# Layer 0 of a graph network with a new order: sums two blocks ahead of the neighbour lists, group steps half a block apart

## The chip, the cores and the metric

The kernel runs on one core of a Trainium2 chip. The metric is the device time of one execution in microseconds (us); lower is better. The engines are PE (TensorE), DVE (VectorE), ACT (ScalarE) and POOL (GpSimd); SP only issues DMAs. Each engine works through its own instructions strictly in the order of the program, and waits for the others by semaphores.

## The reference

Four layers over one graph with 3327 nodes, 256 features and a random adjacency matrix (int32, about 16 neighbours a row).

```python
# layer 0
h = x @ Wt.T + bt                                   # 3327 x 64
s = leaky_relu(h @ Wa.T + ba, 0.2)                  # one score per row
w = softmax(where(adj > 0, s, NEG), axis=1)         # the score of a row is the same for all its neighbours
y = x + (w @ h) @ Wp.T + bp
x = gamma * (y - mean) * rsqrt(var + eps) + beta
# layers 1 to 3
q, k, v = layer_norm(x, g1, be1) @ w_qkv            # 8 heads of 32
x = x + softmax(where(adj, q k / sqrt(32), -inf)) v @ w_proj + b_proj
x = x + gelu(layer_norm(x, g2, be2) @ w1 + b1) @ w2 + b2
```

## The kernel before, in words

Rows are handled in 26 blocks of 128 (`NB`; the last has 127), blocks in 7 groups of four (the last group has two). Everything below happens in layer 0 (`sparse_path`, lines 623 to 1131); layers 1 to 3 follow and gather the neighbours' keys and values row by row with indirect DMAs (L1226). They need two things from layer 0: the table `t1` (rows and neighbour lists) and `perm`, the rows sorted by number of neighbours, by which `t1` is read (L1186).

Per **block** (class `Block`):
- `load` (L696): 1.66 MB of the adjacency matrix go to `a32` (three buffers, DMA on SP); ACT's `sign` (L705) turns them into bf16 `abf` (three buffers), POOL sets the pad columns (L702).
- `turn` (L707): 26 transposes on PE in four chunks (L714), each chunk copied to `aT` by ACT (L715). There are two PSUM buffers for the chunks, and `aT` holds a pair of blocks.
- `candidates` (L717): DVE multiplies `abf` by column numbers (L720) and takes the eight largest of each of 16 segments (L724).
- `list` (L726): DVE takes the 40 largest of these 128 (L735, L737): the neighbour list.

`setup` (L740) turns the weights, brings x to h through PE (`x_turn` L767, `h_of` L779), splits h into three bf16 parts (L805 to L809), and makes the column sum of h (L817, `phsum`) and the scores s (L823 to L827). x itself is loaded by 26 indirect DMAs on POOL (L658).

Per **pair**, `sums` (L838): 52 matmuls of 256 columns add h over the neighbours of 256 rows.

Per **group** (class `Group`) twelve steps: `copy` (L853, ACT), `back` (L860, PE and ACT: sums and degrees with rows on partitions), `soft` (L871, DVE: degrees, one-hot `OH` of the degree, the row's rank among rows of equal degree through PE's `places`, softmax factors; its two exponentials are on ACT, L911), `mix` (L915, DVE), `project` (L933, PE; the bias bp is a matmul with K=1, L944), `add` (L950, DVE: residual, statistics, an inverse root in thirteen small operations), `norm` (L960, DVE), `norm1` (L969, DVE statistics for layer 1), `turn1` (L974, ACT and PE), `qkv(0)` and `qkv(2)` (L982, PE and ACT, two blocks each), `store` (L999, DMA to `t1` on ACT's queue).

Most PSUM results go through `bank`, a pool of three. The order is written out by hand: everything runs in program order, so where a step is called decides where it stands in the queue of each of its engines. In the main loop (L1032 to L1049) a block is loaded one block ahead, turned, then (for even i) the pair before is summed, and then the steps in the list `late` are called one or two at a time between `candidates` and `list`:

```python
turn(i)
if i == 0:
    S.w1 = load_qkv(1, a, bank); setup()
elif i % 2 == 0:
    sums(i - 1)
k = 1 if i < NB - 2 else 2
some(k); blk[i].candidates(); some(k); blk[i].list(); some(k)
```

After the loop comes the sort (L1052 to L1105): prefix sums over degrees (`more`), the rank of each row, its high and low digits (`hib`, `lo`), one-hot matrices (L1089 to L1095) and 26 matmuls (L1098) that give `perm`. The last group's steps stand among and behind it (L1049, L1069, L1075, L1087, L1108). `norm1` uses `Norm` (L566), whose `scale` ends in `nm` (L582) and whose `turn` (L588, L591) and `out` (L596) make the transposed, normalised x.

Of the kernel before, what the change touches and what calls it, by code (L numbers as in the profile page):

```python
# [523 lines left out]
def sparse_path(ctx, tc, ins, out, dram, flag):  # L524
# [98 lines left out]
    with tc.tile_pool(name="a", bufs=1) as a, tc.tile_pool(name="aw", bufs=2) as aw, \  # L623
# [42 lines left out]
        nrow = 3 * D + 2 * H0 + 1  # L666
        row = a.tile([1, nrow], FP, name="s_row")
        o = 0
        for name, n in (("gamma", D), ("beta", D), ("bp", D), ("bt", H0), ("Wa", H0), ("ba", 1)):
            src = ins[f"L0_gnn_{name}"]  # L670
            nc.sync.dma_start(row[:, o:o + n], src if len(src.shape) == 2 else src[None, :])
            o += n
# [15 lines left out]
        places = a_acc.tile([P, 512], FP, tag="places", name="places")  # L688

        class Block:  # L690
# [5 lines left out]
            def load(self):  # L696
                i, r = self.i, self.r
                a32 = aw.tile([P, N], I32, tag="a32", bufs=3, name=f"s_a32_{i}")
                for p0, p1 in (((0, P),) if r == P else ((0, r // 16 * 16), (r // 16 * 16, r))):
                    nc.sync.dma_start(a32[p0:p1], ins["adj"][i * P + p0:i * P + p1, :])  # L700
                self.abf = aw.tile([P, PADDED], BF, tag="abf", bufs=3, name=f"s_abf_{i}")
                nc.gpsimd.memset(self.abf[:, N:], 0.0)  # L702
                if r < P:
                    nc.gpsimd.memset(self.abf[96:P, :], 0.0)
                nc.scalar.sign(self.abf[:r, :N], a32[:r])  # L705
# [11 lines left out]
            def candidates(self):  # L717
                i = self.i
                v = aw.tile([P, NSEG, SEG], BF, tag="v", name=f"s_v_{i}")
                nc.vector.tensor_mul(v, self.abf.rearrange("p (s c) -> p s c", c=SEG),  # L720
                                     seg1[:, None, :].to_broadcast([P, NSEG, SEG]))
                self.cand = aw.tile([P, NSEG, 8], FP, tag="cand", name=f"cand_{i}")
                for s in range(NSEG):
                    nc.vector.max(out=self.cand[:, s, :], in_=v[:, s, :])  # L724
# [15 lines left out]
        def setup():  # L740

            wtT = a.tile([P, 2, H0], FP, name="s_wtT")
            S.wpT = a.tile([H0, D], FP, name="s_wpT")
# [5 lines left out]
            nc.vector.tensor_copy(wtT, pt[:, :2 * H0].rearrange("p (c h) -> p c h", c=2))  # L749
            nc.vector.tensor_copy(S.wpT, pt2[:H0, :D])  # L750
# [7 lines left out]
            S.gam_b, S.bet_b, S.bp_b = (brow[:, k * D:(k + 1) * D] for k in range(3))  # L758
            bt_b = brow[:, 3 * D:3 * D + H0]
            wa_b = brow[:, 3 * D + H0:3 * D + 2 * H0]  # L760
            ba_b = brow[:, nrow - 1:nrow]

            h_sb = aw.tile([P, NB, H0], FP, tag="abf", bufs=3, name="s_h")
            nc.vector.memset(h_sb[96:P, NB - 1, :], 0.0)
            turned = {}

            def x_turn(g):  # L767
                blocks = GROUPS[g]
                xT = aw.tile([P, 2, 512], FP, tag="hT", name=f"s_xT_{g}")
                for c in range(2):  # L770
                    pb = bank(f"s_px_{g}_{c}")
                    for j, i in enumerate(blocks):
                        nc.tensor.transpose(pb[:, j * P:(j + 1) * P],
                                            x_sb[:, i, c * P:(c + 1) * P], ident)
                    (nc.vector.tensor_copy if c else nc.scalar.copy)(
                        xT[:, c, :len(blocks) * P], pb[:, :len(blocks) * P])
                turned[g] = xT

            def h_of(g):  # L779
                blocks, xT = GROUPS[g], turned.pop(g)  # L780
                ph = bank(f"s_ph_{g}").rearrange("p (b h) -> p b h", h=H0)
                for j, i in enumerate(blocks):
                    for c in range(2):
                        nc.tensor.matmul(ph[:, j, :], xT[:, c, j * P:(j + 1) * P],
                                         wtT[:, c, :], start=(c == 0), stop=(c == 1))
                full = [j for j, i in enumerate(blocks) if ROWS[i] == P]
                for j0, j1, r in ((0, len(full), P), (len(full), len(blocks), ROWS[-1])):
                    if j1 > j0:
                        i0 = blocks[j0]
                        nc.vector.tensor_add(  # L790
                            h_sb[:r, i0:i0 + j1 - j0, :], ph[:r, j0:j1, :],
                            bt_b[:r, None, :].to_broadcast([r, j1 - j0, H0]))

            for g in range(len(GROUPS)):
                x_turn(g)
                if g:
                    h_of(g - 1)
            h_of(len(GROUPS) - 1)

# [3 lines left out]
            nc.vector.tensor_copy(hs[:, :, :H0], h_sb)  # L805
            nc.vector.tensor_sub(rest, h_sb, hs[:, :, :H0])
            nc.vector.tensor_copy(hs[:, :, H0:2 * H0], rest)
            nc.vector.tensor_sub(rest, rest, hs[:, :, H0:2 * H0])
            nc.vector.tensor_copy(hs[:, :, 2 * H0:3 * H0], rest)  # L809
            S.fold = a.tile([P, H0], FP, name="s_fold")  # L810
            nc.vector.tensor_copy(S.fold, ident[:, :H0])
            nc.vector.tensor_add(S.fold, S.fold, ident[:, H0:])

            ph = bank("s_phsum")
            for i in range(NB):
                r = ROWS[i]
                nc.tensor.matmul(ph[:, :H0], ones[:r, :], h_sb[:r, i, :],  # L817
# [4 lines left out]

            nc.vector.tensor_mul(rest, h_sb, wa_b[:, None, :].to_broadcast([P, NB, H0]))  # L823
            s = S.s = a.tile([P, NB], FP, name="s_s")
            nc.vector.tensor_reduce(s, rest, AX.X, ALU.add)
            nc.vector.tensor_scalar(s, s, ba_b, None, ALU.add)
            nc.vector.scalar_tensor_tensor(s, s, 0.2, s, ALU.mult, ALU.max)  # L827

        class Group:
# [17 lines left out]

            def steps(self):
                return [self.copy, self.back, self.soft, self.mix, self.project, self.add,
                        self.norm, self.norm1, self.turn1, lambda: self.qkv(0),  # L850
                        lambda: self.qkv(2), self.store]
# [19 lines left out]
            def soft(self):  # L871
# [4 lines left out]
                def sv(name):  # L876
# [10 lines left out]
                                        top[:, :, None].to_broadcast([P, n, nd]), ALU.is_equal)  # L887
                for j in range(n):
                    i = b0 + j
                    nc.tensor.matmul(places[:, :nd], tri, OH[:, i, :], start=(i == 0), stop=True,  # L890
                                     skip_group_check=True)
                    t = aw.tile([P, nd], FP, tag="place", name=f"place_{i}")
                    nc.vector.tensor_mul(t, places[:, :nd], OH[:, i, :])
                    nc.vector.tensor_reduce(rank[:, i:i + 1], t, AX.X, ALU.add)
                    nc.tensor.matmul(places[:, :nd], rest_tri, OH[:, i, :], start=False, stop=True,
                                     skip_group_check=True)
# [36 lines left out]
            def project(self):  # L933
# [4 lines left out]
                nT = aw.tile([H0, 512], FP, tag="nT", bufs=1, name=f"s_nT_{g}")  # L938
                nc.scalar.copy(nT[:, :n * P], pt[:H0, :n * P])
                self.ps = []  # L940
                for j0 in range(0, n, 2):
                    ps = bank(f"s_pp_{g}_{j0}").rearrange("p (b d) -> p b d", d=D)
                    for j in range(2):
                        nc.tensor.matmul(ps[:, j, :], ones[0:1, :], row[:, 2 * D:3 * D],  # L944
                                         start=True, stop=False)
# [622 lines left out]
```

## Time and profile before

| | us |
|---|---|
| median of 3 runs | 2890.99 (2877.77 to 2891.98) |
| profiled execution | 2888.34 |
| its span, first to last instruction | 2886.5 |
| mean granted clock of PE over the span | 0.816 |
| first neighbour list begins (L720) | 75.60 |
| list of block 25 ends | 566.4 |
| perm is written (L1105) | 611.8 |
| first gather from t1 (L1186) | 630.1 |
| busy from 0 to 612: PE, DVE, ACT | 364, 415, 224 |

A span is read from the first to the last instruction of one execution; busy time is the time in which an engine runs instructions; the granted clock says which share of its full speed PE had. A window's row gives the busy time of PE, PE's weight loads, DVE, ACT and POOL with the number of instructions, then the clock, the share of the 16 DMA engines and GB/s. A wait is an engine's idle time before an instruction, with the engine and line that ended it, the total, how often and the longest.

### The profile page before, as it was taken

Reading aid. Unit: us, or ns where it says so; the run is one execution under the profiler, and the core shown is the slowest. Engines: PE = TensorE matmul, PEld = TensorE weight load, DVE = VectorE, ACT = ScalarE, POOL = GpSimd, SP = SyncE. Lnnn points to the kernel's source line nnn. Section 1 sums busy time; section 2 is a strip of 40 time slices with the busy share of each in tenths; the row PEclk is TensorE's granted clock in tenths of the full one; section 3 lists DMA queues with packets and bytes.
Section 4 is the critical chain, followed back from the end, with each engine's and each line's share of the span. In section 5 each row is a group of like instructions: output and inputs, shape, how many; then the busy total and the mean of one; then the engine's idle time right before and its main releaser. Section 6 shows DMA issues by size and latency. Waiting matters only on the chain. (4 is left out here: it accounts for less than half of the span.)

```text
span 2886.5 us, 21905 instructions
## 1 busy us (share of the span) xinstructions
PE 2003.6 (69%) x6391; PEld 1062.0 (37%) x6391; DVE 1981.0 (69%) x4141; ACT 791.8 (27%) x1363; POOL 1359.1 (47%) x1461
## 2 busy tenths in 40 slices
PE   4566666623678887897347878878782678777866
PEld 4344444411334333344213434333350233333334
DVE  2977787447787777773378877777714886778852
ACT  2443443200233332332102323332230023222221
POOL 3000000017776766650377655665405777777740
PEclk9677666756889989898678989988995798888988
DMA  4323331137776766670477656665506776666650
GB/s 179 128 98 119 125 104 52 52 112 217 217 220 197 210 197 188 181 180 16 144 210 210 194 174 178 190 181 155 120 27 189 210 202 194 190 190 188 200 135 15
DMA packets 144480, 453.67 MB, mean 157 GB/s; under 512 B 29522, under 2 KB 40157, under 8 KB 141022
## 3 DMA queue, kind: packets, MB, share of 16 engines
q0 software_dynamic: 113056, 370.26, 45.7%
q1 hardware_dynamic: 9834, 53.90, 5.3%
q10 hardware_dynamic: 21458, 28.02, 2.7%
q8 instruction: 52, 0.85, 0.1%
q14 instruction: 80, 0.65, 0.1%
HBM read 420.64 MB, written 31.42 MB: 157 GB/s over the span
## 5 line engine op out<-in xcount | busy, mean ns | idle before, releaser
L1226 POOL DMA_INDIRECT kv<-kv,t x1344 | 1273.2, 947 | 806.0 <-issue 370.0
L1294 PE MATMUL po<-vw,s_ident 128*128 128x512 f32 (+1 forms) x1380 | 778.2, 700 | 493.5 <-DVE vw L1289 443.6
L1248 DVE TENSOR_TENSOR kv<-kv,q 128x1024 f32<-128x1024 f32 (+3 forms) x363 | 413.4, 1139 | 309.7 <-DMA kv<-kv,t 152.9
L1294 PEld LDWEIGHTS po<-vw,s_ident 128*128 128x128 f32 x1380 | 286.3, 221 | 845.3 <-issue 476.5
L1249 DVE TENSOR_REDUCE sc<-kv 128x32 f32<-128x1024 f32 (+3 forms) x363 | 414.1, 1141 | 12.4
L1289 DVE TENSOR_TENSOR vw<-kv,w 128x1024 f32<-128x1024 f32 x333 | 371.2, 1127 | 0.2
L1373 PE MATMUL pu<-fT,s_w 128*128 128x512 f32 (+3 forms) x768 | 302.4, 527 | 1.0 <-ACT fT L596 1.0
L1396 PE MATMUL py<-gT,s_w 128*128 128x512 f32 (+2 forms) x672 | 283.8, 549 | 0.0
L1379 ACT ACTIVATE gT<-pu,pvb 128x512 f32<-128x512 f32 (+3 forms) x192 | 116.6, 608 | 350.7 <-PE pu L1373 350.2
L702 POOL MEMSET s_abf<- 128x1 bf16 x26 | 2.6, 104 | 435.2 <-PE s_ptb L714 251.6
L1373 PEld LDWEIGHTS pu<-fT,s_w 128*128 128x128 f32 x768 | 147.4, 201 | 136.2 <-issue 111.6
L1396 PEld LDWEIGHTS py<-gT,s_w 128*128 128x128 f32 x672 | 127.8, 192 | 123.1 <-issue 105.4
L714 PE MATMUL s_ptb<-s_ident_bf,s_abf 128*128 128x128 bf16 x676 | 76.5, 291 | 115.7 <-ACT s_aT L715 84.4
L724 DVE MAX8 cand<-s_v 128x8 f32<-128x208 bf16 x416 | 117.5, 360 | 0.9
L714 PEld LDWEIGHTS <-s_abf 128*128 128x128 bf16 x676 | 65.4, 135 | 128.9 <-issue 94.7
L1426 PE MATMUL pk<-s_w_qkv,nT 128*128 128x512 f32 x208 | 106.4, 636 | 8.8 <-ACT nT L596 8.8
L588 ACT ACTIVATE xn_f<-t,nm_f,rqy_f 128x256 f32<-128x256 f32 x78 | 42.9, 593 | 247.6 <-DVE nm_f L582 238.3
L1263 ACT ACTIVATE sc<-sc,mx 128x120 f32<-128x120 f32 (+6 forms) x78 | 31.9, 410 | 260.9 <-DVE mx L1260 257.1
L1334 DVE TENSOR_TENSOR t<-t,po 128x256 f32<-128x256 f32 x78 | 32.5, 417 | 99.7 <-PE po L1330 95.2
L715 ACT COPY s_aT<-s_ptb 128x896 bf16<-128x896 bf16 x104 | 83.3, 853 | 64.6 <-PE s_ptb L714 64.6
L1186 POOL DMA_INDIRECT t<-t,perm x26 | 24.6, 946 | 158.6 <-DMA colsb<-in_L_gnn_be_dram 151.0
L1414 DVE TENSOR_TENSOR t<-t,pd 128x256 f32<-128x256 f32 x75 | 29.5, 408 | 93.3 <-PE pd L1410 93.3
(285 smaller groups left out, 2455.0 us busy)
## 6 DMA issues: line engine op xcount, KB each, us to landing
s_a<-in_adj_dram SPq DMA_DIRECT2D x25, 1663.5 KB
kv<-kv,t POOLq DMA_INDIRECT x1344, 3.8
kv<-kvr ACTq DMA_DIRECT2D x52, 256.0 KB
kv<-s_kvr ACTq DMA_DIRECT2D x26, 256.0 KB
s_w<-in_L_gnn_w_dram SPq DMA_DIRECT2D x6, 1024.0 KB
t<-ql ACTq DMA_DIRECT2D x6, 592.0 KB
t<-s_x ACTq DMA_DIRECT2D x6, 512.0 KB
s_w_qkv<-in_L_gnn_w_qkv_dram SPq DMA_DIRECT2D x3, 768.0 KB
```

Of the source, the lines that this page charges most:

```text
L714: nc.tensor.transpose(pt[:, m, :], self.abf[:, k * P:(k + 1) * P], ident_bf)
L715: nc.scalar.copy(aT[:, k0:k0 + len(ks), :], pt[:, :len(ks), :])
L724: nc.vector.max(out=self.cand[:, s, :], in_=v[:, s, :])
L1226: nc.gpsimd.indirect_dma_start(out=t[:, s, :], out_offset=None, in_=kv[L], in_offset=bass.IndirectOffsetOnAxis(ap=t2[:, b, k:k + 1].bitcas ...
L1248: nc.vector.tensor_mul(k, k, self.q[b][:, None, :].to_broadcast([P, n, D]))
L1249: nc.vector.tensor_reduce(self.sc[b][:, s0:s0 + n, :], k.rearrange("p s (h d) -> p s h d", d=HD), AX.X, ALU.add)
L1289: nc.vector.tensor_mul(vw[:, :n * D].rearrange("p (s h d) -> p s h d", h=HEADS, d=HD), v, self.wp[b][:, s0:s0 + n, :, None].to_broadcast([ ...
L1294: nc.tensor.matmul(self.po[b][:, :m], ident, vw[:, s * D:s * D + m], start=(s0 + s == 0), stop=(s0 + s + 2 >= S), skip_group_check=True)
L1373: nc.tensor.matmul(c["pu", f][:, :n], w["w1"][:, e, f * P:(f + 1) * P], c["hT"][:, e, :n], start=(e == 0), stop=(e == 1))
L1379: nc.scalar.activation(g[:, :n], c.pop(("pu", f))[:, :n], AF.Gelu_apprx_tanh, bias=w["b1"][:, f:f + 1])
L1396: nc.tensor.matmul(c["py"][e][:, :n], w["w2"][:, f, e * P:(e + 1) * P], g[:, :n], start=(f == 0), stop=last)
L1426: nc.tensor.matmul(ps[:, :c1 - c0], c["hT"][:, e, j * P:(j + 1) * P], nxt["w_qkv"][:, e, c0:c1], start=(e == 0), stop=(e == 1))
```

## The change

Layer 0 computes the same, with these edits.

- **Start.** Blocks 0 to 2 are loaded, signed and turned first; blocks 0 and 1 get their lists before the weights are turned. `setup` is split into `weights0`, `split_h` and `of_h`; the turns of x are called with pieces of the candidates and lists of blocks 2 and 3 between them. h lies in an `a32` buffer instead of an `abf` buffer. The pad columns of the first three blocks are set on DVE.
- **Lead.** In round i block i+2 is loaded, signed and turned, and the pair that ends with i+2 is summed, while block i gets its list.
- **Group steps by a plan.** A table gives the half round in which each step is called; steps are mostly one half round apart, with two from `back` to `soft`.
- **soft.** The four blocks of a group are ranked with one product and one sum over 4 x 41 columns; PE adds up all earlier blocks' counts (`ones_bf`, `rest_tri`) into four regions of `places`, which are cleared once by a matmul with zeros.
- **norm** is done by ACT in one instruction per block; gamma and beta follow on DVE, once per group, in `norm1`.
- **bp** becomes a 65th row of the projection weights, with a row of ones in `nT`; the K=1 matmuls go. Some copies (`wtT`, `wpT`, half of `xT`) go from DVE to ACT.
- **End.** The last group's `soft`, `mix` and `project` are in the last round; `add`, `norm`, `norm1`, `turn1`, `qkv` and `store` are placed before the one-hot part of the sort.

```diff
-                nc.scalar.sign(self.abf[:r, :N], a32[:r])
+            def sign(self):
...
+                (nc.vector if i < 3 else nc.gpsimd).memset(self.abf[:, N:], 0.0)
...
+                nc.scalar.sign(self.abf[:r, :N], self.a32[:r])
...
                 for j in range(n):
                     i = b0 + j
-                    nc.tensor.matmul(places[:, :nd], tri, OH[:, i, :], start=(i == 0), stop=True,
-                                     skip_group_check=True)
-                    t = aw.tile([P, nd], FP, tag="place", name=f"place_{i}")
-                    nc.vector.tensor_mul(t, places[:, :nd], OH[:, i, :])
-                    nc.vector.tensor_reduce(rank[:, i:i + 1], t, AX.X, ALU.add)
-                    nc.tensor.matmul(places[:, :nd], rest_tri, OH[:, i, :], start=False, stop=True,
-                                     skip_group_check=True)
+                    add = [(tri, i)] + [(ones_bf, k) for k in range(b0, i)]
+                    if g:
+                        add += [(rest_tri, i - 4)] + [(ones_bf, k) for k in range(i - 3, b0)]
+                    for lhsT, m in add:
+                        nc.tensor.matmul(at[:, j, :], lhsT, OH[:, m, :], start=False, stop=True,
+                                         skip_group_check=True)
+                t = aw.tile([P, 4, nd], FP, tag="place", bufs=1, name=f"place_{g}")[:, :n]
+                nc.vector.tensor_mul(t, at[:, :n, :], OH[:, b0:b0 + n, :])
+                nc.vector.tensor_reduce(rank[:, b0:b0 + n], t, AX.X, ALU.add)
...
-                        nc.tensor.matmul(ps[:, j, :], ones[0:1, :], row[:, 2 * D:3 * D],
-                                         start=True, stop=False)
-                        nc.tensor.matmul(ps[:, j, :], nT[:, (j0 + j) * P:(j0 + j + 1) * P], S.wpT,
-                                         start=False, stop=True)
+                        nc.tensor.matmul(ps[:, j, :], S.nT[:, (j0 + j) * P:(j0 + j + 1) * P], S.wpT,
+                                         start=True, stop=True)
...
             def norm(self):
...
-                    nc.vector.scalar_tensor_tensor(xi, xi, self.n0.mv[:, j, 0:1], S.gam_b,
-                                                   ALU.subtract, ALU.mult)
-                    nc.vector.scalar_tensor_tensor(xi, xi, self.n0.rs[:, j:j + 1], S.bet_b,
-                                                   ALU.mult, ALU.add)
+                    nc.scalar.activation(xi, xi, AF.Identity, bias=self.n0.nm[:, j:j + 1],
+                                         scale=self.n0.rs[:, j:j + 1])
 
             def norm1(self):
+                n, b0 = self.n, self.blocks[0]
+                xg = x_sb[:, b0:b0 + n, :]
+                nc.vector.tensor_mul(xg, xg, S.gam_b[:, None, :].to_broadcast([P, n, D]))
+                nc.vector.tensor_add(xg, xg, S.bet_b[:, None, :].to_broadcast([P, n, D]))
...
+        for i in range(3):
+            blk[i].load()
+        for i in range(3):
+            blk[i].sign()
             turn(i)
...
+        for i in range(2):
             blk[i].candidates()
             blk[i].list()
+        S.w1 = load_qkv(1, a, bank)
+        weights0()
+        blk[3].load()
+        blk[3].sign()
...
+        for g in range(NG):
+            x_turn(g)
+            if g:
+                h_of(g - 1)
+            if g == 2:
+                turn(3)
+            if g == 4:
+                blk[4].load()
+                blk[4].sign()
+            for _ in range(2 if g > 3 else 1):
+                pieces.pop(0)()
+        h_of(NG - 1)
+        split_h()
+        sums(1)
+        of_h()
+        turn(4)
+        sums(3)
+        groups[0].copy()
+        blk[5].load()
+        blk[5].sign()
+        turn(5)
+        sums(5)
...
+        for g in reversed(range(NG)):
+            at = dict(zip(names, (0, 1, 3, 4, 5, 6, 7, 8, 9, 10, 11, 12)))
+            first = 8 * g + 4
+            if g == 0:
+                first = 8
+                at["copy"] = -9
+                at["back"] = 0
+            elif g == NG - 2:
+                at.update(norm=6, norm1=7, turn1=7, qkv0=99, qkv2=99, store=99)
+            elif g == NG - 1:
+                first = 2 * NB - 4
+                at.update(soft=2, mix=3, project=3, add=99, norm=99, norm1=99, turn1=99, qkv0=99,
+                          qkv2=99, store=99)
...
+        for i in range(4, NB):
+            if i + 2 < NB:
+                blk[i + 2].load()
+                blk[i + 2].sign()
+            for s in plan[2 * i]:
+                step(*s)
+            blk[i].candidates()
+            if i + 2 < NB:
+                turn(i + 2)
+                if i % 2 or i + 2 == NB - 1:
+                    sums(i + 2)
+            for s in plan[2 * i + 1]:
+                step(*s)
+            blk[i].list()
+        last = groups[-2:]
+        last[0].qkv(0)
+        last[0].qkv(2)
+        last[0].store()
```

In the sort, `last[1].add()` and `norm()` now stand behind `wide`, and `norm1()`, `turn1()`, `qkv(0)` and `store()` behind `num_bf`, ahead of `oh_lo`; the calls of `some` are gone.

## The prediction

> **What bounds the kernel now.** I first read the 40 slices of the page for where the gathering begins.
>
> ```profile
> DVE  2977787447787777773378877777714886778852
> POOL 3000000017776766650377655665405777777740
> ```
>
> A slice is 72 us. POOL loads x in slice 1 and is then empty until slice 9, where layers 1 to 3 begin to gather. So layer 0 stands by itself, nothing of the later layers overlaps it, and what its end moves, the whole moves. The timeline of its end says when, and on what:
>
> ```profile
> 580.49 0.17 DVE L882 COPY deg<-s_acc 128x2 f32<-128x2 f32 x1 [13.93 <-ACT s_acc L869]
> ...
> 628.58 0.07 DVE L1154 MEMSET least<- 128x8 f32 x1 [9.87 <-DMA t<-s_x]
> ```
> ```profile
> 630.10 0.97 POOL L1186 DMA_INDIRECT t<-t,perm  x1 [151.00 <-DMA colsb<-in_L_gnn_be_dram]
> ```
>
> The first gather starts at 630.1, right after the last group's store has landed (628.6), 18 us after perm is written (611.8). From there to the end are 2886.5 - 630.1 = 2256.4 us, which the diff doesn't touch. Next come the stretches (PE, PEld, DVE, ACT, POOL busy, clock, DMA share, GB/s):
>
> ```profile
> 14.50:75.60 61.10, 34.70 (x257) 30.85 (x258) 19.54 (x31) 13.71 (x17) 17.64 (x20) 0.98 0.38 147
> 75.60:566.00 490.40, 308.58 (x1743) 218.95 (x1743) 369.35 (x1347) 201.48 (x238) 5.20 (x24) 0.68 0.27 96
> 566.00:612.00 46.00, 20.68 (x122) 13.75 (x120) 23.59 (x81) 4.48 (x12) 0.00 (x0) 0.67 0.17 52
> ```
>
> DVE is the fullest engine but is idle for 41 of the first 61 us, for a quarter of the main stretch and for half of the end; DMA and ACT have room. The waits of DVE from 75 to 612 name what holds it:
>
> ```profile
> DVE deg L882 <- ACT s_acc L869: 92.8, 6, 19.1
> DVE s_x L955 <- PE s_pp L946: 21.0, 8, 5.0
> ```
>
> In each group soft() is called right after back(), so DVE stands still while PE goes through transposes, sums and back. The starts of the blocks' first DVE instruction (L720) give the rhythm: 75.60 for block 0, 235.35 for block 10, 314.96, 393.78 and 474.07 for blocks 14, 18, 22: **79.6 us for four blocks**.
>
> **Costs on DVE, by its own pitch.** One block's list is 10.2 us (the step between L720 starts of blocks 0 to 4): candidates 6.5, list 3.7. A group of four in the new form:
> - soft: OH and its inputs 0.6; one product and one sum over 128x164 instead of four of each over 128x41 (0.20 each). No row has the PSUM product; it lies between 0.20 (128x41) and 0.42 (128x256), and I take 0.33 from OH (L885, the same 164), so 0.7; twelve small ones 1.7 (582.3 to 583.95). Sum 3.1.
> - mix 2.6 (L919 to L931), add 6.0 (sums 1.4, statistics 2.1, root 2.5), store 0.2.
> - norm leaves DVE (52 instructions of 0.48) for ACT: four of 0.59 (L588's row) per group. In exchange norm1 gets two passes over 128x1024, 1.14 each by L1248's row: 2.3 + 4.7 = 7.0.
>
> So 18.9 per group where it was 21.6, and a cycle of four blocks is 40.8 + 18.9 = **59.7 us without a wait**.
>
> **Costs on PE.** The bias product of K=1 goes: 26 blocks x 1.15 (L944, two records of 0.573) = 30 us less. The places matrices go from 2 to 5 matmuls a block, 20 a group; back to back such a pair is 0.03 apart (365.85, 365.87) and one alone reads 0.20, so 0.6 to 4; I take 1. Whether that matters depends on the clock:
>
> ```profile
> 300.00:302.00 2.00, 2.00 (x5) 0.99 (x4) 1.79 (x9) 0.24 (x1) 0.00 (x0) 0.50 0.62 100
> 302.00:304.00 2.00, 2.00 (x5) 0.94 (x4) 1.83 (x7) 0.00 (x0) 0.00 (x0) 0.50 0.82 333
> ...
> 312.00:314.00 2.00, 2.00 (x21) 1.90 (x19) 1.93 (x5) 0.00 (x0) 0.00 (x0) 1.00 0.00 0
> 318.00:320.00 2.00, 0.00 (x0) 0.00 (x0) 2.00 (x9) 0.00 (x0) 0.00 (x0) 0.61 0.00 0
> ```
>
> PE busy through 300 to 304 has a clock of 0.50, in the sums at 312 it has 1.00, and 2 us after they end the clock falls. A sums call of 52 matmuls takes 6.9 (309.07 to 315.95), its first twelve at 0.213 a step and the rest at 0.109; the same call takes 11 cold and 5.7 warm.
>
> **Step by step: the start, 0 to block 10 (before: 235.35).** Block 0 is signed at 14.5 as before; DVE now starts its list there, since the pad columns are set by DVE and no longer by POOL behind the x loads (L702 at 38.3). Blocks 0 and 1: 14.5 + 20.4 = 35. On ACT sign and turn alternate for blocks 0 to 2, to 34; the weights take both to 38 (38.7 to 43.6 before); sign(3) 3 us, then the x turns at 2.62 a group (the step of L773), with turn(3) (3.4, four L715) and sign(4) (3.0) among them: 43 + 18.4 + 6 = 67. The pieces of blocks 2 and 3 on DVE (20.4) and the additions fit between. split_h takes 7.0 as before: 74. Here is a new queue on PE: sums(1) 7, phsum 6.0, turn(4) 3.5, sums(3) 6, so 96.5; copy(0) and then sign(5) on ACT end at 101, while DVE is through with of_h (4.7) and block 4 at 89: **a wait of 12**. Then turn(5), sums(5), back(0), turns 6 and 7 and sums(7) hold PE to 130, and soft(0) waits for its places matmuls behind them: DVE's block 5 ends its candidates at 107.5, so 20 more. From 130: rest of soft and list(5) 6; rounds 6 to 9 are four lists 40.8, mix twice 5.2, add twice 12, soft(1) 3.1, norm1(0) 7, waits 3. Block 10 starts at **207**, 28 earlier.
>
> **The middle, blocks 10 to 21 (before: 238.7).** In a round the order is sign(i+2), first steps, candidates(i), turn(i+2) with the sums when i is odd, second steps, list(i). I set DVE's start of a cycle at 0. norm1(g-1) ends at 7, xn and hT on ACT take 4.5 (485.1 to 489.8 before), qkv0 on PE 6.8 (335.7 to 342.5), turn 3.5, sums 6 to 7, places 1: PE is there at 28.6 to 30. DVE has done two candidates, a list and OH at 24.4: **soft waits 5**. Behind it PE does qkv2 and turn, and project (1.0, a copy of 0.6 and four of 1.15) ends at 49.7 against DVE's 48.4 + 0.7: 1 more. Everything else has over 5 us in hand: signs are two blocks ahead, ACT has 40 us of work in the cycle. So 66. The first cycle finds qkv2(0) still before it and waits 5 more: 71 + 66 + 66 = **203**, 36 earlier.
>
> **The end, block 22 to the first gather (before 630.10 - 474.07 = 156.0).** Rounds 22 to 25: 17.2, 13.3, 13.0 and 28.0 (soft(6), add(5), mix(6), norm1(5) and the block), waits 6: 77.5. Behind the last list: store 0.2, ranks 4.7, wide 0.4, add(6) 4.3, high digits 2.2, a wait of 3.5 as norm(6) on ACT stands behind four blocks of qkv(5), norm1(6) 5.0: 20.3. From the last group's nm_q to the first gather it was 630.10 - 615.64 = 14.5 and stays so; the one-hot sort (5.6) and perm now lie beside it. 77.5 + 34.8 = **112**, 44 earlier.
>
> **Sum.** 207 + 203 + 112 + 2256.4 = 2778.4 of span; the profiled execution has 2888.34 - 2886.5 = 1.8 around it: **2780 us**, 108 below its own 2888.3. That execution lies 2.7 under the median of 2890.99; I give the sum as it is.
>
> **A rule against the trace.** The clock rises some 2.5 us into the sums and is gone a few us after they end, while the K=1 and K=64 products of project (299.6 to 305.9) stay at 0.50. The Trainium skill (TensorE: Matmul & The Clock Gate, Part 1) says that about 3.4 us of sustained activity release the clock and an idle window of that length takes it back. The sums agree with that; project, busy for twice as long, does not. By the rule project would be 2 us shorter and the wait of 1 gone, 2777; the row is what I use.
>
> **Rivals.**
> - *DVE never waits.* If PE is warm at qkv0 and sums, soft's wait goes: middle 3 x 59.7 = 179 (24 less), end 6 less, start 8 less: 2742. For it: PE has 52 us busy in a cycle of 80 now, and 6 us of K=1 go. Against it: qkv0, turn and sums are one queue ahead of places. 14%.
> - *PE stays cold.* At 0.50 qkv0 is 10.4 (3.7 + 1.5 for the block at 494.8, twice), turn 5.2 (its transposes at 329.2 and 334.4, 1.7 and 1.5, and two copies), sums 11: PE reaches places at 39.4, soft waits 15 and project 3, a cycle is 78. Middle 234 (31 more), end 10 more, start 15 more: 2836. The clock is 0.68 now. 16%.
> - *x comes late.* POOL still issues x while DVE now works. At 644.95 and 646.48 two gathers (L1226) took 1.22 and 1.33 instead of 0.95 while DVE copied (L1178, L1179); beside L1248 they kept 0.95. If lists hold POOL up as copies do, the 17 issues left at 14.5 end up to 18 us later, of which the x turns, begun with the first groups, pass on 5 to 18: 2785 to 2798. The Trainium skill (SBUF — State Buffer, Who interferes with whom) gives the mechanism, a shared port, and names copies and casts as holding it, products of two inputs as not; by that it is 0. 5%.
> - *Slower: the order ties the engines together.* soft's exp on ACT stands ahead of the next sign and turn, so ACT and PE can't run past DVE. If a share f of PE's cold work per cycle (turns 21, sums 22, qkv 21, project 6, back and turn1 8: 78) lies open on DVE, a cycle is 59.7 + 78 f. The order of before leaves (79.6 - 62.4)/78 = 22% open; the 108 us of the forecast are lost over 4 cycles when one is 93 instead of 66, f = 43%. At 50% it is 98.7: 2780 + 4 x 32.7 = 2911. Against it: two blocks of lead in sign and turn. 4%; with 1% near no change.
> - That the change doesn't reach the end: only if the gather waits for something that does not move. The weights of layer 1 are issued at 629.4 too, behind the same release. Included in the forecast's spread.
>
> **Numbers.** Forecast 60%, the others as above. The range is 2740 to 2832: below by DVE without waits, above by most of the cold case; the rest, some 2 in 10, lies outside. About 0.5% (14 us) can be told from no change: faster 95%, same 1%, slower 4%.
>
> **What would show it.** First gather near 522; DVE over 85% busy from 130 to 500; no wait for s_acc; a wait for places of about 5 us per group; first list at 14.5; the stretch behind the first gather 2256 within 10. I am wrong in the middle if the four-block step isn't 62 to 72, in the start if block 10 is not within 195 to 220, in the end if block 22 to the gather isn't 105 to 125.

## The result and the profile after

The changed kernel takes 2781.7 us (median of 4 runs, 2777.0 to 2783.7), the kernel before beside it 2887.3 (4 runs, 2877.8 to 2892.0): a ratio of 0.9636, 95% interval 0.9606 to 0.9666. The profiled execution took 2781.14 us with a span of 2779.3. The forecast was 2780.

The 40 slices of the page after (a slice is now 69.5 us), DVE and POOL:

```profile
DVE  6597888577877777733788677778427878778852
POOL 4000000377766666601776565566017777776741
```

POOL's empty stretch ends in slice 8 instead of 9, and from there on the row has much the shape that it had. The whole gain lies ahead of the first gather. Its timeline, DVE and POOL:

```profile
518.85 0.14 DVE L1203 TENSOR_SCALAR worst<-before 1x1 f32<-1x1 f32 x1
519.25 0.07 DVE L1226 MEMSET least<- 128x8 f32 x1 [0.26 <-DVE worst L1203]
```
```profile
519.85 0.98 POOL L1258 DMA_INDIRECT t<-t,perm  x1 [99.28 <-DVE bias L1229]
```

The first gather starts at 519.8, where it was 630.1: 110.3 earlier. Behind it are 2259.5 us, where there were 2256.4. What DVE waits for from 0 to 530 in the changed kernel (total, times, longest):

```profile
DVE place L906 <- PE places L903: 41.1, 7, 16.2
DVE s_v L731 <- ACT s_abf L714: 22.3, 2, 11.9
DVE s_h L804 <- PE s_ph L798: 12.8, 4, 5.8
DVE s_x L981 <- ACT s_x L975: 6.2, 2, 5.2
DVE pf L1177 <- PE pp_perm L1173: 4.9, 1, 4.9
DVE deg L889 <- ACT s_acc L876: 4.7, 1, 4.7
```

The 92.8 us of s_acc have become 4.7, and the 21.0 of s_pp are gone. What is left is named differently: places, the small matmuls in the middle of soft, and sign in the start. The stretches (PE, PEld, DVE, ACT, POOL busy, clock, DMA share, GB/s):

```profile
74.00:133.50 59.50, 45.11 (x390) 40.30 (x390) 25.95 (x62) 22.94 (x23) 0.20 (x2) 0.82 0.32 116
...
209.00:408.50 199.50, 147.18 (x968) 112.59 (x967) 168.61 (x608) 116.30 (x144) 1.22 (x12) 0.78 0.40 136
408.50:519.80 111.30, 57.55 (x268) 35.58 (x267) 91.42 (x343) 30.70 (x57) 2.97 (x2) 0.68 0.16 51
```

DVE is busy 85% of the middle now, but only 44% of the stretch from 74 to 133.5: there DVE still stands idle for 33 us.

### The profile page after: what moved, and what is told of

The parts are those of the page before. It is cut to its first block, busy times and chain, and to the rows that moved or that the text cites. A ratio compares the mean times of both kernels' runs of the same rounds, so it can differ in the third digit from the quotient of the medians.

```text
span 2779.3 us, 21889 instructions
## 1 busy us (share of the span) xinstructions
PE 1952.0 (70%) x6409; PEld 1045.3 (38%) x6409; DVE 1961.9 (71%) x4061; ACT 806.5 (29%) x1398; POOL 1361.8 (49%) x1458
## 5 line engine op out<-in xcount | busy, mean ns | idle before, releaser
L1366 PE MATMUL po<-vw,s_ident 128*128 128x512 f32 (+1 forms) x1380 | 770.4, 694 | 497.4 <-DVE vw L1361 447.6
L1320 DVE TENSOR_TENSOR kv<-kv,q 128x1024 f32<-128x1024 f32 (+3 forms) x363 | 413.3, 1139 | 312.6 <-ACT q L1306 156.5
L1366 PEld LDWEIGHTS po<-vw,s_ident 128*128 128x128 f32 x1380 | 285.3, 220 | 846.5 <-issue 468.3
L1445 PE MATMUL pu<-fT,s_w 128*128 128x512 f32 (+3 forms) x768 | 308.1, 536 | 1.0 <-ACT fT L596 1.0
L723 PE MATMUL s_ptb<-s_ident_bf,s_abf 128*128 128x128 bf16 x676 | 69.8, 273 | 77.3 <-ACT s_abf L714 64.0
L588 ACT ACTIVATE xn_f<-t,nm_f,rqy_f 128x256 f32<-128x256 f32 x78 | 42.9, 593 | 247.5 <-DVE nm_f L582 240.1
L723 PEld LDWEIGHTS <-s_abf 128*128 128x128 bf16 x676 | 58.8, 125 | 91.8 <-ACT s_abf L714 70.8
L855 PE MATMUL s_pa<-s_aT,s_hs 128*128 128x256 bf16 x338 | 80.4, 286 | 13.2 <-DVE s_hs L817 13.2
```

The costliest lines, as they stand in the source:

```text
L723: nc.tensor.transpose(pt[:, m, :], self.abf[:, k * P:(k + 1) * P], ident_bf)
L1320: nc.vector.tensor_mul(k, k, self.q[b][:, None, :].to_broadcast([P, n, D]))
L1366: nc.tensor.matmul(self.po[b][:, :m], ident, vw[:, s * D:s * D + m], start=(s0 + s == 0), stop=(s0 + s + 2 >= S), skip_group_check=True)
L1445: nc.tensor.matmul(c["pu", f][:, :n], w["w1"][:, e, f * P:(f + 1) * P], c["hT"][:, e, :n], start=(e == 0), stop=(e == 1))
```

## The experiments

For every kernel I read the same five times from its trace: the first DVE instruction of block 10 (L731; L720 in the kernel before), the three steps of four blocks from there to block 22, block 22 to the first gather, the first gather, and the rest of the span. Each row of the table is read from one execution; after_again is the changed kernel once more on another chip, and its first gather differs by 0.7. In the changed kernel norm1 of a group (7.2 us of DVE) stands just ahead of that instruction of block 10 and of block 22. In lead_one and lead_one_with_back it stands a round later: their column of block 10 holds 7.2 less than it would like for like, and the one from 22 to the gather 7.2 more. In combo_switch it stands a round later up to block 14.

| kernel | block 10 | steps of four | 22 to gather | first gather | rest | ratio to before (95%) |
|---|---|---|---|---|---|---|
| before | 235.4 | 79.6, 78.8, 80.3 | 156.0 | 630.1 | 2256.4 | |
| changed | 216.6 | 73.0, 63.5, 62.5 | 104.3 | 519.8 | 2259.5 | 0.9636 (0.9606 to 0.9666) |
| after_again | 216.5 | 72.0, 62.0, 63.5 | 105.2 | 519.1 | 2256.7 | 0.9620 (0.9604 to 0.9637) |
| work_only | 217.6 | 75.2, 75.1, 75.1 | 151.7 | 594.7 | 2741.5 | 0.9898 (0.9852 to 0.9944) |
| order_only | 226.2 | 77.7, 67.6, 68.3 | 102.9 | 542.7 | 2745.0 | 0.9735 (0.9695 to 0.9774) |
| soft_with_back | 223.3 | 75.9, 71.1, 68.4 | 108.0 | 546.7 | 2734.8 | 0.9775 (0.9730 to 0.9820) |
| late_pieces | 212.5 | 72.0, 62.0, 63.4 | 105.2 | 515.2 | 2747.4 | 0.9671 (0.9631 to 0.9710) |
| lead_one | 191.2 | 63.4, 63.6, 62.5 | 115.2 | 496.0 | 2255.6 | 0.9529 (0.9514 to 0.9545) |
| lead_one_with_back | 199.5 | 68.5, 69.9, 68.7 | 123.1 | 529.6 | 2263.7 | 0.9649 (0.9626 to 0.9673) |
| split_soft | 217.7 | 71.3, 59.3, 60.2 | 102.1 | 510.6 | 2256.3 | 0.9577 (0.9561 to 0.9593) |
| early_group0 | 207.4 | 62.7, 63.5, 62.5 | 104.3 | 500.4 | 2263.2 | 0.9558 (0.9535 to 0.9582) |
| combo_two | 196.3 | 59.8, 59.3, 60.2 | 94.9 | 470.5 | 2260.7 | 0.9445 (0.9418 to 0.9471) |
| combo_switch | 182.2 | 67.4, 66.6, 60.8 | 95.2 | 472.2 | 2270.5 | 0.9477 (0.9456 to 0.9497) |
| combo_late_pieces | 205.8 | 59.8, 60.6, 59.3 | 94.2 | 479.7 | 2250.8 | 0.9483 (0.9456 to 0.9510) |

work_only, order_only, soft_with_back and late_pieces ran on a chip on which everything behind the first gather took some 485 us longer (the kernel before took 3379.1 there); ahead of it the times are the same as elsewhere, so their ratios are not comparable with the others and I compare first gathers. That this is sound is seen in the differences: on that chip the four medians are 37.2, 91.2, 82.4 and 114.1 below the one of before, and their first gathers are 35.4, 87.4, 83.4 and 114.9 ahead of the 630.1 of before.

**Work or order?** work_only puts the new pieces into the order of the kernel before, order_only the old pieces into the new order.

```
# work_only: the loop of before, calling the new steps
+            k = 1 if i < NB - 2 else 2
+            some(k)
             blk[i].candidates()
+            some(k)
             blk[i].list()
...
-            for s in plan[2 * i]:
-                step(*s)
...
+            some(k)
# order_only: the new plan, calling the old steps
-                nc.vector.tensor_mul(t, at[:, :n, :], OH[:, b0:b0 + n, :])
...
+                    nc.vector.tensor_mul(t, places[:, :nd], OH[:, i, :])
...
+                        nc.tensor.matmul(ps[:, j, :], ones[0:1, :], row[:, 2 * D:3 * D],
+                                         start=True, stop=False)
...
-                    nc.scalar.activation(xi, xi, AF.Identity, bias=self.n0.nm[:, j:j + 1],
-                                         scale=self.n0.rs[:, j:j + 1])
+                    nc.vector.scalar_tensor_tensor(xi, xi, self.n0.mv[:, j, 0:1], S.gam_b,
+                                                   ALU.subtract, ALU.mult)
```

> The order of the kernel before (sums one block ahead, each group's steps one after another, last groups behind the sort) with the new pieces: one places product per group, bias as the 65th row, first norm on ACT, copies of the start on ACT. Theory (the order makes the gain): DVE does 2.7 us less per group (18.9 for 21.6), 18 in all, and of its 21.0 us of waits for the projection some 12 go with the K=1 products; the 92.8 us of waits for the sums taken back (s_acc) stay within 15 of that. 2888 - 30 = 2858, between 2835 and 2875. Rival (the work makes the gain): the s_acc waits shrink by half or more, below 2820.

> The new order with the old pieces: places block by block, K=1 bias products, both norm passes on DVE. Theory (order): DVE 2.7 us more per group (18), places in turns between PE and DVE 5, and the K=1 products (4.6 a group) against some 3.4 us that PE has in hand at the additions, 8: 2781 + 31 = 2812, between 2795 and 2825. Rival (work): above 2850.

work_only's first gather is at 594.7, 35.4 earlier than before; order_only's at 542.7, 87.4 earlier. Together they would be 122.8, 12.5 more than the two of them do in one kernel; the start's copies on ACT are in both kernels, so some is counted twice. The rival (the work) fell. In work_only DVE waits for the sums as long as it did:

```profile
DVE deg L889 <- ACT s_acc L876: 91.1, 6, 18.4
```

A step of four blocks is 75.1 there instead of 79.6: the lighter steps are worth 4.5 of the 16 to 17 that a later step of the changed kernel gains, the order the rest (order_only's later steps are 67.6 and 68.3).

**Soft in the same half step as back.**

```
-            at = dict(zip(names, (0, 1, 3, 4, 5, 6, 7, 8, 9, 10, 11, 12)))
+            at = dict(zip(names, (0, 1, 1, 4, 5, 6, 7, 8, 9, 10, 11, 12)))
...
-                at["back"] = 0
+                at["back"] = at["soft"] = 0
...
```

> The changed kernel with soft called in the same half step as back, as closely as in the kernel before. Theory S (the half steps between back and soft carry the middle's gain): DVE waits again for s_acc, up to 15 us a group; the step of four blocks goes from 63 to about 76 and the whole to about 2840. Theory L (the lead of two blocks carries it): in the changed kernel s_acc(3) is there at 283.9 and DVE would call soft at 296, so no wait for s_acc in the middle; the step of four blocks stays at 60 to 66, and the whole within 2770 to 2795.

Neither theory held in full. The step of four blocks is 68 to 76, between the two, and the first gather 27 later than in the changed kernel: 6.8 of it by block 10, 16.5 in the middle, 3.6 in the end. Theory L was right that s_acc would be there (9.0 us of waits from 209 to 500, in 2). But a new wait came, s_pp with 29.2 in 7. ACT and DVE around one of them:

```profile
309.63 0.20 ACT L926 ACTIVATE s_m<-s_m 128x4 f32<-128x4 f32 x1 [15.63 <-DVE s_m L924]
...
309.84 1.08 ACT L588 ACTIVATE xn_q<-s_x,nm_q,rqy_q 128x256 f32<-128x256 f32 x2
```
```profile
345.90 0.69 DVE L967 TENSOR_TENSOR s_x<-s_x,s_pp 128x512 f32<-128x512 f32 x1 [9.54 <-PE s_pp L958]
```

soft's exp (L926) now stands on ACT ahead of the normalised rows of the group before (L588), whose statistics DVE had finished at 299.2. ACT stands still for 15.6 us, the last 10.3 of them with those statistics ready; qkv starts at 313.8, and the projection, further down PE's queue, is 9.5 late. The half steps keep an instruction that waits for DVE out of the way of ACT's other work.

**One block of lead instead of two, with and without those half steps.** With these two the four cases of lead and spacing are complete. All group steps come a round later with them, so the distance from a group's sums to its steps stays, and the last steps of groups 5 and 6 move behind the loop.

```
-            first = 8 * g + 4
+            first = 8 * g + 6
...
-            if i + 2 < NB:
-                blk[i + 2].load()
-                blk[i + 2].sign()
+            if i + 1 < NB:
+                blk[i + 1].load()
+                blk[i + 1].sign()
...
-                turn(i + 2)
-                if i % 2 or i + 2 == NB - 1:
-                    sums(i + 2)
...
+                turn(i + 1)
+                if i % 2 == 0 or i + 1 == NB - 1:
+                    sums(i + 1)
...
```

> The changed kernel with sign, turn and sums one block ahead of the lists instead of two, all group steps a round later, the half steps between them kept. Theory S (the spacing carries the middle's gain): the step of four blocks stays at 62 to 67, and the end is 5 to 15 longer since the last group's steps come a round later; first gather at 525 to 540. Theory L (the lead carries it): the step goes to 72 to 80, DVE waits for s_abf or s_acc; first gather at 560 to 590.

> The kernel of lead_one (sums one block ahead) with soft in the same half step as back. With this the four cases of lead and spacing are complete. Theory S (the half steps between back and soft carry the middle's gain, the lead nothing): the step of four blocks goes from 63.5 to 70 to 78, as in the kernel with the old order and the new work (75.1), with DVE waits for s_acc or s_pp; first gather at 515 to 545. Rival (something else in the old order cost it, such as one place of the steps in the round): 63 to 66, first gather within 6 of 496.

lead_one takes 23.2 us off the first gather of the changed kernel (496.0 for 519.1 on the same chip). The second block of lead is not what makes the gain; it costs. Step of four blocks, behind the first one:

| | soft two half steps behind back | soft with back |
|---|---|---|
| lead of two | 63.5, 62.5 | 71.1, 68.4 |
| lead of one | 63.4, 63.6, 62.5 | 68.5, 69.9, 68.7 |

The columns differ by 6, the lines by next to nothing. In lead_one_with_back too the wait of the three steps is the one for the projection (7.5, 8.4 and 7.9), and ACT stands still ahead of exp for 9.9, 17.0 and 17.2 us:

```profile
330.85 0.69 DVE L967 TENSOR_TENSOR s_x<-s_x,s_pp 128x512 f32<-128x512 f32 x1 [8.36 <-PE s_pp L958]
```

The expected 70 to 78 for lead_one_with_back was a little high: work_only's 75.1 holds some 6 more than spacing. There soft comes in the very round of its group's last sums, and DVE waits for s_acc; in all kernels with the plan the sums lie a round ahead of soft, and none of them has that wait of 15 us in each group. That this round is worth the other 6 is argued: no run takes it away alone. What the second block of lead costs is seen in the waits of lead_one up to its first gather, beside those of the changed kernel above:

```profile
DVE s_v L731 <- ACT s_abf L714: 22.0, 2, 11.6
DVE place L906 <- PE places L903: 21.8, 7, 6.4
```

The wait for places is half as long, and the one for s_acc has gone. In the changed kernel turn(5) and sums(5) stand on PE ahead of back(0), and turn(6), turn(7) and sums(7) as well ahead of the places of soft(0); with one block of lead nothing stands ahead of the one, and turn(5), sums(5) and turn(6) ahead of the other. At block 22 lead_one is 33.2 ahead of after_again and its end is 10.0 longer, but 7.2 of both is the norm1 that it still has before it. Like for like it is 26.0 ahead there (18.1 of it by block 10), and its end is 2.8 longer.

**The places matmuls half a step earlier.** split_soft cuts soft in two, and PE gets the places behind qkv0 and ahead of turn and sums.

```
+        for k, todo in enumerate(plan):
+            for g, name in list(todo):
+                if name == "soft" and 0 < g < NG - 1:
+                    todo[todo.index((g, name))] = (g, "soft_b")
+                    plan[k - 1].append((g, "soft_a"))
```

> The changed kernel with soft in two: one-hot and places matmuls half a step earlier, behind qkv0 of the group before and ahead of turn and sums on PE; the product that reads them where soft was. Theory: the waits for places are PE's queue (turn and sums, 7 to 10 us) and not work; 13.6 of the first cycle falls to about 5, some 4 in each later one to 0: first gather 12 to 20 earlier than in the changed kernel. Rival (PE is as full as DVE in the cycle, the wait comes back at the projection or at sign): less than 5 earlier, with new waits for s_pp or s_abf.

8.6 earlier than after_again, under the 12 to 20. The later steps did what was expected, 59.3 and 60.2 where DVE's own work is 59.7 by the prediction's sum. In the first step the wait moved to the projection, as the rival had it (s_pp 7.2 in 3): there PE really was behind. So the wait of a later step was order, that of the first was work left over from the start.

**Group 0 earlier.**

```
+        h_sum()
         split_h()
...
+        blk[5].load()
+        blk[5].sign()
         sums(3)
         groups[0].copy()
...
+        blk[4].candidates()
+        groups[0].back()
+        blk[4].list()
+        groups[0].soft()
         turn(5)
         sums(5)
+        blk[6].load()
+        blk[6].sign()
+        turn(6)
...
```

h_sum makes the column sum of h (26 products on PE), which stood in of_h; the loop over the blocks begins at 5.

> The changed kernel with another start: the sum over h on PE while DVE splits h, block 5 signed ahead of sums(3), back(0) and soft(0) ahead of turn(5) and sums(5), group 0's later steps a round earlier. Theory: the 33 us that DVE waits between 93 and 133 stem from the order on PE and ACT; of them 12 (sign) go, and 16 + 5 (places and acc of group 0) shrink to about 3: block 10 starts 20 us earlier, between 12 and 30, and so does the first gather. Rival (PE's work of the start, 85 of the 135 us from 74 to 209, sets it): less than 8.

18.7 earlier than after_again, as the theory had it, but not where: block 10 is only 9.1 earlier, since the projection of group 0 now stood behind turn(7) and sums(7). The other 9 are the first step, 62.7 instead of 72.0: what PE had carried over from the start was gone.

```profile
DVE s_x L969 <- PE s_pp L960: 15.8, 2, 15.7
...
DVE place L908 <- PE places L905: 15.1, 7, 4.1
```

**The lists while x arrives.** late_pieces takes the lists of blocks 2 and 3 out of the x turns and puts them behind the first sums; combo_late_pieces does the same to combo_two (below).

```
-            for _ in range(2 if g > 3 else 1):
-                pieces.pop(0)()
...
         of_h()
+        for piece in pieces:
+            piece()
```

> The changed kernel with the lists of blocks 2 and 3 moved from among the x turns to behind the first sums. Theory: DVE waits 33 us between 93 and 133 for PE's queue, so the 20.4 us of lists are hidden there as well: block 10 starts within 4 us of 209, the whole between 2777 and 2787. Rival (the early lists make the start's gain): 20 later, 2801.

> combo_two with the lists of blocks 2 and 3 moved from among the x turns to behind the first sums, the same edit as in late_pieces. Theory: early lists pay as much as DVE then works on without a wait. In the changed kernel 33 us of waits took them up; in combo_two 20 us of waits are left from 83 to 207 (10.3 for sign, 6.0 for acc, some 4 for s_pp), and 5 to 15 more are got back among the x turns: of the 20.4 us of lists 5 to 14 come back, first gather at 475 to 485. Rival (the early lists are worth nothing in any of these orders): within 3 of 470.5. Other rival (they are worth all of it): 488 to 492.

late_pieces' first gather is 4 to 5 earlier than the changed kernel's (515.2 for 519.1 and 519.8), so these 20.4 us of lists earn nothing there: DVE waits for PE's queue anyway. In combo_two, where those waits are gone, the same edit costs 9.2 (479.7 for 470.5), within the 5 to 14. The medians of the two (2733.5 and 2734.6) don't show it, since the stretch behind the first gather happened to differ by 9.9 the other way. The ratios to before lean that way (0.9445 and 0.9483), but their intervals overlap; the 9.2 rest on one execution of each.

**All of it.** combo_two joins split_soft and early_group0 (its projection ahead of turn(7)) and changes the end: add(6) and norm(6) ahead of the four blocks of qkv(5), norm1(6) ahead of the sort's digits, the sort's check in the wait for pp_perm. combo_switch has a lead of one up to block 12 and of two behind it.

```
         last = groups[-2:]
+        last[1].add()
+        last[1].norm()
         last[0].qkv(0)
         last[0].qkv(2)
...
-        last[1].add()
-        last[1].norm()
...
+        last[1].norm1()
         hib = aw.tile([P, NB, NB], BF, tag="abf", bufs=3, name="hib")
```

> Lead of two, with the early group 0 (its projection now ahead of turn(7) and sums(7)), soft in two, and another end: add(6) and norm(6) ahead of the four blocks of qkv(5), norm1(6) ahead of the sort's digits, the sort's check in the wait for pp_perm. Theory: early group 0 18.7 less, three steps of four blocks at 60 instead of 63, 10, the end's soft 3, the end's two waits (5.2 and 4.9) 8, the wait for s_pp of group 0 (15.7) half, 8: first gather at 471, between 463 and 485. Rival (PE is as full as DVE once these waits are gone): the edits don't add up, 490 or more.

> As combo_two, but sums one block ahead up to block 12 and two ahead from there: the start of lead_one with the end of the changed kernel. Theory: the lead of two costs in the start (lead_one starts block 10 25.3 earlier) and pays only in the end (10): first gather 5 to 15 earlier than in combo_two, at 460 to 475, with no wait over 6 for s_pp in the start. Rival (the early group 0 has already taken what the lead costs): within 4 of combo_two.

combo_two's first gather is at 470.5, 48.7 earlier than after_again's. Its median is 2733.5 us beside 2896.0 for the kernel before on the same chip. DVE's largest waits up to the first gather are

```profile
DVE s_h L804 <- PE s_ph L798: 11.6, 4, 4.5
DVE s_v L731 <- ACT s_abf L714: 10.3, 1, 10.3
DVE s_x L978 <- PE s_pp L969: 7.8, 4, 5.9
DVE deg L895 <- ACT s_acc L878: 6.0, 1, 6.0
```

and from 189 to 368 it is busy 168.0 of 179.0 us. combo_switch gains nothing on it (472.2), as its rival had it, but not quite for the rival's reason. At block 10 it is still 6.9 ahead of combo_two like for like (14.1 less the 7.2 of norm1), where lead_one was 18.1 ahead of after_again: the early group 0 had taken most of what the second block costs in the start. The 6.9 are lost in the step from block 10 to 14 (67.4 for 59.8), where the switch puts the signs and turns of two blocks into one round and DVE waits for the projection:

```profile
243.39 0.69 DVE L978 TENSOR_TENSOR s_x<-s_x,s_pp 128x512 f32<-128x512 f32 x1 [6.29 <-PE s_pp L969]
```

Whether another way of switching would keep the 6.9 was not tried.

## Why the prediction was right, point by point

The mechanism held: the wait for s_acc went, and each stretch came out near its forecast. That the sum is within a microsecond or two is luck, since the errors of the four stretches (2 and 3 too short, 4 and 1 too long) cancel.

- **Where the time is**: right. Layer 0 stands alone ahead of the first gather, so its end moves the whole: 110.3 of first gather, 107.2 of span.
- **The start**: 207 expected for the round of block 10, 209.3 measured (216.55 less the 7.2 of norm1). The two waits were expected at 12 and 20, and were 11.9 (sign(5)) and 4.7 + 16.2 = 20.9 (acc and places of group 0). The account of PE's queue ahead of soft(0) is what made this right. What it left out are DVE's waits for the x turns (s_ph, 12.8 in 4): split_h ended at 78.7 instead of 74, and the rounds up to block 10 gave half of that back.
- **The middle**: 71 + 66 + 66 = 203 expected, 73.0 + 63.5 + 62.5 = 199 measured. DVE's own 59.7 holds: split_soft, which takes the wait out, has 59.3 and 60.2. The wait for places was put at 5, and at 10 in the first step: it was 13.6, then 4.1 and 3.1. The wait of 1 for the projection did not come. So the first step was sized too short and the two later ones too long. In the first step I named qkv2(0) as what still stands before. It does, and more comes behind it:

```profile
231.47 3.64 PE L1005 MATMUL s_pk<-s_w_qkv,s_hT 128*128 128x512 f32 x4 [0.65 <-ACT s_hT L596]
...
233.49 0.33 DVE L892 TENSOR_TENSOR OH<-num,s_top 128x164 bf16<-128x164 f32 x1
...
246.70 0.18 PE L903 MATMUL places<-OH,tri 128*128 128x41 bf16 x1
...
247.41 0.33 DVE L906 TENSOR_TENSOR place<-places,OH 128x164 f32<-128x164 f32 x1 [13.59 <-PE places L903]
```

  qkv0(1) itself was late. The statistics for its xn were ready on DVE at 216.5, but ACT was with qkv2(0) until 217.5 and then had sign(12) and the copies of group 2's sums, of turn(12) and of back(2) to do, so that xn started at 227.5. early_group0 takes that away, and the first step falls to 62.7.
- **The end**: 112 expected, 111.3 measured, with errors that cancel. Waits of 5.2 (norm(6) behind qkv(5); expected 3.5) and of 4.9 (pp_perm behind qkv(6) on PE, not foreseen) stand against waits of 3.2 for places where 6 were expected. The first gather came 15.0 behind nm_q(6), expected 14.5, but another thing released it: not the store of the last group but the end of the sort's check on DVE (519.0, behind it the line at 519.25 above). In combo_two, where that check comes earlier, it is the store again.
- **The rest**: 2256.4 expected, 2259.5 measured; without any edit there it lies between 2250.8 and 2263.7 in most of the runs, 2270.5 in one.
- **DVE never waits** (2742): not this kernel, but combo_two, which reaches 59.3 to 60.2 a step and 2733.5. The condition that the prediction gave, PE warm at qkv0 and sums, was half met here: of qkv0 the first four products took 3.78 us, others of that kind 1.88, but the sums from 304.5 on took 5.7, the warm time, and DVE still waited 4.1 for places. It isn't what took the wait away in combo_two, where the clock from 189 to 368 is 0.80, for 0.77 here. There places go ahead of turn and sums; split_soft changes nothing else and has the 59.3 and 60.2.
- **x comes late**: its mechanism showed, too small to matter. Three of the 26 issues took longer on POOL, each beside a product of a list on DVE (1.84, 2.38 and 3.69 where the kernel before has 0.95, 0.95 and 2.55; the last takes 2.56 in late_pieces, where no list stands beside it):

```profile
14.58 1.89 DVE L731 TENSOR_TENSOR s_v<-s_abf,seg 128x3328 bf16<-128x3328 bf16 x1 [10.37 <-ACT s_abf L714]
15.45 1.84 POOL L658 DMA_INDIRECT s_x<-in_x_dram,rows_i  x1 [0.30 <-issue]
24.79 1.88 DVE L731 TENSOR_TENSOR s_v<-s_abf,seg 128x3328 bf16<-128x3328 bf16 x1
25.11 2.38 POOL L658 DMA_INDIRECT s_x<-in_x_dram,rows_i  x1 [0.30 <-issue]
```

  Both issues end 0.82 us after the product beside them. So this product of two inputs held them up, which by the rule that the prediction quotes it should not; the searches for the largest (MAX8) beside the other issues did not (0.95 each). The last issue ends at 40.2, where it ended at 38.3, and DVE never waited for x.
- **Slower, the order ties the engines together**: not in the changed kernel, but its mechanism is real, as soft_with_back shows (ACT still for 15.6 us ahead of exp). Against it the prediction set two blocks of lead. That reason fell: with one block the step is the same. What keeps the engines apart is the half steps between back and soft, worth 6 a step.
- **What I took for granted**: that each part named in the change earns something. The early lists of blocks 2 and 3 earn nothing, the second block of lead costs 26.0 up to block 22 and gives 2.8 back in the end. By the size of the first gather's move, order_only has 87 of the 110.

## What to carry to other kernels

An instruction that waits for another engine stands in front of everything behind it in its queue: place it half a step later than its input, and ahead of long work that nobody waits for yet. Work moved into an idle stretch is earned only if the next stretch has no wait that would have hidden it; the same 20.4 us of lists were worth less than nothing in one order and 9 in another. Read the first stretch after a pipeline starts on its own: running further ahead cost more there than it gave later.

## What the runs showed of the hardware

- One chip ran the same code behind the first gather in 2735 to 2747 us, where others took 2251 to 2271, with layer 0 unchanged. In late_pieces there DVE's products have the same mean as in the changed kernel's own run (L1320: 1138 and 1139 ns), and 1344 gathers issue in the same 950 and 947 ns. Part of the difference shows as waits without a named releaser: those of PE's weight loads ahead of L1366 add up to 728.7 us, the longest 35.3, for 468.3 and 13.0. The cause stays open.
- The clock did not follow PE's load in the way that I had used. From 256 to 266 PE was busy for 8.68 of 10 us at a clock of 0.50, and the projection took 3.78; from 318 to 326 it was busy for 5.36 of 8 at a clock of 0.79, and the same eight products took 2.00:

```profile
256.00:266.00 10.00, 8.68 (x49) 7.02 (x50) 9.59 (x33) 7.05 (x8) 0.10 (x1) 0.50 0.75 253
262.00:264.00 2.00, 2.00 (x6) 1.63 (x5) 1.83 (x8) 2.00 (x1) 0.00 (x0) 0.50 0.59 233
264.00:266.00 2.00, 2.00 (x14) 1.56 (x13) 1.79 (x10) 0.26 (x2) 0.00 (x0) 0.50 0.56 106
318.00:326.00 8.00, 5.36 (x38) 4.23 (x38) 7.86 (x23) 7.16 (x7) 0.10 (x1) 0.79 0.86 279
```

  The Trainium skill (TensorE: Matmul & The Clock Gate, Part 1) has some 3.4 us of sustained activity release the clock. This trace does not agree: it stayed at 0.50 from 262 to 266, where PE shows busy throughout, and in the kernel before from 296 to 306, with 2.00 of 2.00 us busy in each row. What tells these stretches from the sums, which did get the full clock, stays open. Neither case delayed DVE, which waited for no projection in this kernel.
